# A hybrid transformer block: batch 0's residual, layer norm and first experts given out in attention a's last four periods

## The chip, the cores and the metric

The kernel runs on one core of one Trainium2 chip. The metric is device time in microseconds for one launch, the median of several runs. All arithmetic is in float32; two of the matmul operands are stored in the fp32r form.

## What is computed

Input x has 2 batches of 512 positions and 512 channels. Four layers follow one another, each with a layer norm ahead of it and a residual around it:

```python
x = x + attn_a(layernorm(x))    # 32 heads of 128, 8 kv heads, weights as 4-bit codes and scales
x = x + ffn(layernorm(x))       # 8 experts of rank 64, the best 2 of a softmax gate
x = x + attn_b(layernorm(x))    # 32 heads of 16, 8 kv heads
x = x + ffn(layernorm(x))       # the same experts again

def ffn(x):                     # x as 1024 rows
    gate_probs = softmax(x @ gate_w.T)
    weights, sel = top_k(gate_probs, 2)
    weights = weights / sum(weights)
    w_full = zeros(T, N_EXPERTS).at[arange(T)[:, None], sel].add(weights)
    for e in range(N_EXPERTS):
        out = out + w_full[:, e:e + 1] * (x @ lora_A[e].T @ lora_B[e].T)
```

Both attentions are causal and rotary. The change touches the place where the first line ends and the second begins.

## The kernel before

A program (a tile framework) assigns semaphores and places. It also orders the instructions on each engine when the kernel is built: in program order by preference, with later work drawn forward where its operands are there and the engine would be free. In the loop of attention b, TensorE's order is fixed by hand instead. Tiles come from pools; a pool's tag has a number of buffers, and pools opened later may lie on the place of pools that have been closed.

**Attention a** (lines 128 to 378). A unit is one head of one batch: 64 units in the order group g, batch b, head h, so units 60 to 63 are batch 1's last four and 56 to 59 batch 0's. The loop at line 335 has 68 periods. Period n gives out, in turns of one step each (`in_turn`, line 302), the following work on different units: `weighted` for unit n-3 (four groups of transposes L275 with their copies L276, then the av group of eight matmuls L280), `rotated` for unit n (query projection L209 and L210, evicted by L214 and L216, and the rotary L225 to L228), `output` for unit n-4 (L289 and L290, added to `acc` by L296 to L299), `softmaxed` for unit n-2 (scores L247, maxima L250 on VectorE, exponentials L255 on ScalarE, scaling L264 on GpSimd), and some steps of keys and values of the next group. From period 64 there are no projections any more, from 66 no scores, and period 67 has only the outputs of unit 63. `acc[0]`, batch 0's sum, is complete after period 63.

The pools of attention a, in order: `w` (4 buffers of converted weights, queries and outputs of two groups), `wkv` (2, keys and values), `xa` (the normalised input in two parts, and `acc`), `kv`, `tabs`, `rope` (tags rq, rsq, part and others), `qT`, `p`, `pT`, `attnT`; in PSUM two banks each of `ps_mm` (projections), `ps_sc` (scores), `ps_tp` and `ps_o`.

**Between.** After the loop the residual is added (L375 transposes `acc`, L376 adds it to x), for batch 0 and then batch 1. The pools of attention a are closed, and those of the rest opened: `w2` with `gw`, `fold`, the expert weights `la` and `lb`, and attention b's weights `wq2`, `wkv2`, `wo2` and `tabb`, loaded by SyncE's queue (L386 to L410); the padded tiles for queries, keys and values, cleared by GpSimd (L426 to L432).

**Experts and attention b.** `experts(b, which, store)` is a generator whose steps are: layer norm (`norm_parts`: one step with the statistics L460 and L461, the square root L463, then four tiles with L470, transposes L475 and copy L476), gate (`pg`, L494), first rank block (`ph`, L504, four steps), gate logits and softmax (`lg`, L514 to L521), the choice of two (L529 to L546, all on VectorE), three more rank blocks (twelve steps), the weights spread over the ranks and transposed (`we` L552, `wT` L556, L558; four steps), and the second matmul (`py`, L563, sixteen steps, with the addition to x at L567). Each is 43 steps. First `experts(0, "f1", False)` runs alone (line 784). Then `projections(0)` of attention b is given out in turn with `experts(1, "f1", False)`, which goes on as side work in attention b's loop, at a pace of 1.35 units a step.

```python
    run(experts(0, "f1", False))

    later, now = experts(1, "f1", False), projections(0)
    parts(later, 1)
    while next(now, None) is not None:
        parts(now, 1)
        parts(later, 1)
```

Of the kernel before, what the change touches and what calls it, by code (L numbers as in the profile page):

```python
# [11 lines left out]
F32 = mybir.dt.float32  # L12
I32 = mybir.dt.int32
F32R = mybir.dt.float32r
AF = mybir.ActivationFunctionType
# [26 lines left out]
def kernel(  # L42
# [80 lines left out]


# [3 lines left out]
    with ExitStack() as actx:  # L128
        wpool = actx.enter_context(tc.tile_pool(name="w", bufs=4))
        wkvp = actx.enter_context(tc.tile_pool(name="wkv", bufs=2))  # L130
# [7 lines left out]
        atp = actx.enter_context(tc.tile_pool(name="attnT", bufs=2))  # L138
        ps_mm = actx.enter_context(tc.tile_pool(name="ps_mm", bufs=2, space=PSUM))
        ps_sc = actx.enter_context(tc.tile_pool(name="ps_sc", bufs=2, space=PSUM))  # L140
        ps_tp = actx.enter_context(tc.tile_pool(name="ps_tp", bufs=2, space=PSUM))
        ps_o = actx.enter_context(tc.tile_pool(name="ps_o", bufs=2, space=PSUM))
# [57 lines left out]
        acc = {b: xp.tile([P, NC, S], F32, tag=f"acc{b}", name=f"acc_{b}") for b in range(B)}  # L200
# [105 lines left out]

        kTs, vs = {}, {}
# [27 lines left out]
        for n in range(len(units) + 4):  # L335
# [30 lines left out]
            turn.append(some(more, 3 + (units[min(n, 63)][0] == 0)))  # L366
            in_turn(*turn)

        for b in range(B):
            load_x("r", b, big, "big")  # L370
        for b in range(B):
            for t in range(NT):
                tp = ps_tp.tile([P, NC, P], F32, tag="tp", name=f"px_{b}_{t}")
                for n in range(NC):
                    nc.tensor.transpose(tp[:, n, :], acc[b][:, n, ts(t, P)], ident)  # L375
                nc.vector.tensor_tensor(  # L376
                    x[b, t], x[b, t], tp.rearrange("p n f -> p (n f)"), ALU.add
                )
# [4 lines left out]

    gw = w2.tile([P, NC, STRIP], F32, tag="gw", name="gw")
    nc.gpsimd.memset(gw, 0.0)
    nc.sync.dma_start(gw[:, :, :NE], gate_w)  # L386

    fold = w2.tile([P, NE], F32, tag="fold", name="fold")
    nc.vector.tensor_reduce(
        fold, ident.rearrange("p (c e) -> p e c", e=STRIP)[:, :NE, :], AX.X, ALU.add  # L390
    )
    la = w2.tile([P, NC, NE * RANK], F32, tag="la", name="la")
    nc.sync.dma_start(la, lora_a.rearrange("(c p) n -> p c n", p=P))
    lb = w2.tile([P, NC, DM], F32, tag="lb", name="lb")
    nc.sync.dma_start(lb, lora_b.rearrange("(c p) n -> p c n", p=P))
# [3 lines left out]
    nc.sync.dma_start(wkv2, wkv_b.rearrange("(c p) n -> p c n", p=P))  # L399

# [7 lines left out]

    tabb = w2.tile([P, NT, 4, B_HD], F32, tag="tabb", name="tabb")
    nc.sync.dma_start(tabb, rope_b)  # L410

# [24 lines left out]
    gate = ctx.enter_context(tc.tile_pool(name="gate", bufs=1))  # L436
# [6 lines left out]
    ps_f = ctx.enter_context(tc.tile_pool(name="ps_f", bufs=2, space=PSUM))  # L443

    shared = {"on": True}

    def bank(shape, name):
        pool, tag = (ps_x, "x") if shared["on"] else (ps_f, "f")
        return pool.tile(shape, F32, tag=tag, name=name)

    MM = 0.9
    def norm_parts(b, which):

        var = small.tile([P, NT, 2], F32, tag="mv", name=f"mv_{which}_{b}")
        for t in range(NT):
            st = small.tile([P, 6], F32, tag="st", name=f"st_{which}_{b}_{t}")
            nc.vector.bn_stats(st, x[b, t])  # L460
            nc.vector.bn_aggr(var[:, t, :], st)  # L461
        std = small.tile([P, NT], F32, tag="std", name=f"std_{which}_{b}")
        nc.scalar.activation(std, var[:, :, 1], AF.Sqrt, bias=eps)  # L463
        rstd = small.tile([P, NT], F32, tag="rstd", name=f"rstd_{which}_{b}")
        nc.vector.reciprocal(rstd, std)
        yield 7.0
        xT = xtp.tile([P, NC, S], F32, tag="xnT", name=f"xnT_{which}_{b}")
        for t in range(NT):
            xn = temps.tile([P, DM], F32, tag="t", name=f"xn_{which}_{b}_{t}")
            nc.vector.tensor_scalar(  # L470
                xn, x[b, t], var[:, t, 0:1], rstd[:, t : t + 1], ALU.subtract, ALU.mult
            )
            pt = bank([P, NC, P], f"pxT_{which}_{b}_{t}")
            for c in range(NC):
                nc.tensor.transpose(pt[:, c, :], xn[:, ts(c, P)], ident)  # L475
            nc.scalar.copy(xT[:, :, ts(t, P)], pt)  # L476
            yield MM
        return xT

    def experts(b, which, store):  # L480

        xT = yield from norm_parts(b, which)
        nm = f"{which}_{b}"

        def st(tag, n=1):
            return gate.tile([P, NT, n], F32, tag=tag, name=f"{tag}_{nm}")

        def each(a):
            return a.to_broadcast([P, NT, NE])


        pg = bank([P, S], f"pg_{nm}")
        for c in range(NC):
            nc.tensor.matmul(pg[ts(c, STRIP)], gw[:, c, :], xT[:, c, :], start=True, stop=True)  # L494
        shares = temps.tile([P, S], F32, tag="t", name=f"shares_{nm}")
        nc.scalar.copy(shares, pg)
        yield MM
        hT = hp.tile([P, NC, S], F32, tag="hT", name=f"hT_{nm}")

        def ranks(er):  # L500

            ph = bank([P, S], f"ph_{nm}_{er}")
            for c in range(NC):
                nc.tensor.matmul(  # L504
                    ph, la[:, c, ts(er, P)], xT[:, c, :], start=(c == 0), stop=(c == NC - 1)
                )
                if c == NC - 1:
                    nc.scalar.copy(hT[:, er, :], ph)
                yield MM

        yield from ranks(0)
        lg = bank([P, NT, NE], f"lg_{nm}")
        for t in range(NT):
            nc.tensor.matmul(lg[:, t, :], shares[:, ts(t, P)], fold, start=True, stop=True)  # L514
        mx, pr, den, rden = st("gmx"), st("gp", NE), st("gden"), st("grden")
        nc.vector.tensor_reduce(mx, lg, AX.X, ALU.max)
        nc.vector.tensor_tensor(pr, lg, each(mx), ALU.subtract)
        nc.scalar.activation(pr, pr, AF.Exp)
        nc.vector.tensor_reduce(den, pr, AX.X, ALU.add)
        nc.vector.reciprocal(rden, den)  # L520
        nc.vector.tensor_tensor(pr, pr, each(rden), ALU.mult)  # L521
        yield MM


        best, hot = [], []
        left = pr
        for n in range(2):
            m, key, km, oh = st(f"m{n}"), st(f"key{n}", NE), st(f"km{n}"), st(f"oh{n}", NE)
            nc.vector.tensor_reduce(m, left, AX.X, ALU.max)  # L529
            nc.vector.tensor_tensor(key, left, each(m), ALU.is_equal)  # L530
            nc.vector.tensor_tensor(
                key, key, order.unsqueeze(1).to_broadcast([P, NT, NE]), ALU.mult
            )
            nc.vector.tensor_reduce(km, key, AX.X, ALU.max)
            nc.vector.tensor_tensor(oh, key, each(km), ALU.is_equal)
            best.append(m)
            hot.append(oh)
            if n == 0:
                left = st("left", NE)
                nc.vector.scalar_tensor_tensor(left, oh, -2.0, pr, ALU.mult, ALU.add)  # L540
        tot, rtot, w = st("tot"), st("rtot"), st("gw", NE)
        nc.vector.tensor_tensor(tot, best[0], best[1], ALU.add)
        nc.vector.reciprocal(rtot, tot)
        nc.vector.tensor_tensor(w, hot[0], hot[1], ALU.add)
        nc.vector.tensor_tensor(w, w, pr, ALU.mult)
        nc.vector.tensor_tensor(w, w, each(rtot), ALU.mult)  # L546
        for er in range(1, NC):
            yield from ranks(er)
        for t in range(NT):

            we = wep.tile([P, NE, RANK], F32, tag="we", name=f"we_{nm}_{t}")
            nc.gpsimd.tensor_copy(we, w[:, t, :].unsqueeze(2).to_broadcast([P, NE, RANK]))  # L552
            wef = we.rearrange("p e r -> p (e r)")
            tp = bank([P, NC, P], f"wT_{nm}_{t}")
            for er in range(NC):
                nc.tensor.transpose(tp[:, er, :], wef[:, ts(er, P)], ident)  # L556
            part = hT[:, :, ts(t, P)]
            nc.vector.tensor_tensor(part, part, tp, ALU.mult)  # L558
            yield MM
        for t in range(NT):  # L560
            py = bank([P, DM], f"py_{nm}_{t}")
            for c in range(NC):
                nc.tensor.matmul(  # L563
                    py, hT[:, c, ts(t, P)], lb[:, c, :], start=(c == 0), stop=(c == NC - 1)
                )
                if c == NC - 1:
# [368 lines left out]
```

## Time and profile before

| | |
|---|---|
| median of 3 runs | 1170.47 us (1168.96 to 1172.08) |
| the profiled execution: time | 1172.71 us |
| the profiled execution: span of the core | 1170.7 us |
| TensorE (PE) busy | 1107.2 us, 95% of the span |
| VectorE (DVE) busy | 883.0 us, 75% |
| ScalarE (ACT) busy | 591.7 us, 51% |
| GpSimd (POOL) busy | 525.5 us, 45% |
| mean granted TensorE clock | 0.975 |

All durations come from the profiled execution. A span is from its first to its last instruction; times such as "at 722.3" are microseconds from the span's start. PEld is the weight load, which runs beside matmuls. One float32 matmul is two instructions in the trace. In rows of groups and chains, L504 is line 504 of the kernel, "x8" the number of instructions, and the two numbers ahead are start and length. In rows of stretches the number in brackets counts instructions, and the last three are clock, DMA share and GB/s. In rows of waits, the numbers are the sum, the number of waits, and the longest.

### The profile page before, as it was taken

To read this page: it belongs to the slowest core of one execution; us is meant where nothing else is said; L and a number is where in the kernel's file an instruction comes from. 1 tells how busy PE (TensorE), PEld (TensorE's weight loads), DVE (VectorE), ACT (ScalarE), POOL (GpSimd) and SP (SyncE) were. 2 spreads that over 40 slices of the span, in tenths; PEclk is the share of its full clock that TensorE was granted. 3 is DMA by queue.
4 is the path that set the end of the run, shared out by engine and by line. 5 is a ranking of instruction groups with operands and counts; after the bars stand their busy time and mean duration, and the time that the engine had idled before them with its cause. 6 is when DMAs were issued, how large, how long until landed. Compare 5 with 4: busy or idle time off the path is not lost.

```text
span 1170.7 us, 16843 instructions
## 1 busy us (share of the span) xinstructions
PE 1107.2 (95%) x5428; PEld 694.0 (59%) x5428; DVE 883.0 (75%) x2175; ACT 591.7 (51%) x1373; POOL 525.5 (45%) x758
## 2 busy tenths in 40 slices
PE   5799999999999999999999996989999999999998
PEld 3467777777777776777777774444444444444343
DVE  6889899998998999999998887244755676565442
ACT  3566566576656656656566663212254444364410
POOL 1556655665565666566565665111123322222200
PEclk9999999999999999999999998899989978989999
DMA  7301011022001100101100002400000000000000
GB/s 274 108 1 37 1 37 37 1 72 72 3 35 37 37 1 37 38 1 37 37 1 1 1 1 92 76 0 1 2 1 6 6 6 6 7 6 2 15 32 36
DMA packets 13448, 35.07 MB, mean 30 GB/s; under 512 B 4081, under 2 KB 5041, under 8 KB 10801
## 3 DMA queue, kind: packets, MB, share of 16 engines
q1 hardware_dynamic: 13360, 34.01, 8.8%
q8 instruction: 43, 0.70, 0.2%
q14 instruction: 45, 0.36, 0.1%
HBM read 30.72 MB, written 2.10 MB: 28 GB/s over the span
## 4 chain that ended last, share of the span: by engine, by line
PE 86%; DVE 7%; ACT 2%; POOL 2%; issue 2%; DMA 1%; SPq 0%; DVEq 0%; ACTq 0%; POOLq 0%
PE av L280 11%; PE sc L247 11%; PE st_b L694 7%; PE tp L275 6%; PE ps_o L289 5%; PE ps_o L290 5%; PE ps_q L209 5%; PE py_f L563 5%; PE ps_q L210 5%; PE ph_f L504 4%; PE num_b L721 4%; PE po L764 3%; PE pq_b L603 3%; PE sc_b L668 2%; PE ps_k L210 1%
## 5 line engine op out<-in xcount | busy, mean ns | idle before, releaser
L672 DVE CUSTOM_DVE_ANT_0 sc_b<-sc_b,tri 128x128 f32<-128x128 f32 (+3 forms) x256 | 122.6, 510 | 92.2 <-PE sc_b L668 76.6
L255 ACT ACTIVATE p<-sc,nmx 128x128 f32<-128x128 f32 (+3 forms) x256 | 135.5, 529 | 93.9 <-DVE nmx L250 91.8
L247 PE MATMUL sc<-kT,qT 128*128 128x128 f32 (+3 forms) x512 | 179.6, 433 | 1.5 <-POOL qT L228 1.2
L216 DVE SCALAR_TENSOR_TENSOR r_q<-ps_q,s_q,r_q 128x512 f32<-128x512 f32 x192 | 143.7, 749 | 35.8 <-PE ps_q L210 22.4
L227 POOL TENSOR_TENSOR r_q<-r_q,tab 128x512 f32<-128x512 f32 x64 | 82.3, 1286 | 191.1 <-DVE rs_q L226 191.1
L276 ACT COPY pT<-tp 128x128 f32<-128x128 f32 (+3 forms) x256 | 109.3, 427 | 102.2 <-PE tp L275 101.5
L264 POOL TENSOR_SCALAR p<-p,rden 128x128 f32<-128x128 f32 (+3 forms) x256 | 139.2, 556 | 46.2 <-DVE rden L262 22.8
L704 POOL TENSOR_SCALAR_AFFINE_SELECT pT_b<-pT_b 128x128 f32<-128x128 f32 (+1 forms) x192 | 62.7, 331 | 195.2 <-ACT pT_b L700 192.5
L280 PE MATMUL av<-pT,v 128*128 128x512 f32 (+3 forms) x512 | 148.7, 433 | 0.2 <-ACT pT L276 0.2
L280 PEld LDWEIGHTS av<-pT,v 128*128 128x128 f32 x512 | 96.8, 190 | 80.6 <-issue 52.7
L700 ACT ACTIVATE pT_b<-st_b 128x384 f32<-128x384 f32 (+1 forms) x192 | 92.2, 528 | 96.3 <-PE sc_b L668 68.1
L299 DVE SCALAR_TENSOR_TENSOR acc<-ps_o,s_o,acc 128x512 f32<-128x512 f32 x186 | 137.7, 740 | 2.9 <-PE ps_o L290 2.7
L209 PE MATMUL ps_q<-xh,w_q 128*128 128x512 f32 x256 | 122.8, 480 | 7.4 <-DVE r_q L216 7.4
L250 DVE CUSTOM_DVE_ANT_0 sc<-sc,tri 128x128 f32<-128x128 f32 (+3 forms) x256 | 125.7, 491 | 3.5 <-PE sc L247 2.5
L694 PE MATMUL st_b<-qT_b_p,kT_b 32*128 32x256 f32 (+3 forms) x512 | 119.1, 503 | 6.0 <-DVE qpad L672 3.6
L668 PE MATMUL sc_b<-kT_b,qT_b_m 32*128 32x384 f32 (+3 forms) x512 | 118.2, 499 | 1.4 <-ACT qT_b_m L639 0.7
L275 PE MATMUL tp<-ident,p 128*128 128x128 f32 x640 | 112.7, 272 | 2.3 <-POOL p L264 2.3
L247 PEld LDWEIGHTS sc<-kT,qT 128*128 128x128 f32 x512 | 95.3, 189 | 24.3 <-POOL qT L228 1.6
L289 PE MATMUL ps_o<-ah,w_o 128*128 128x512 f32 x256 | 108.3, 424 | 1.1 <-ACT ah L168 0.9
L290 PE MATMUL ps_o<-al,w_o 128*128 128x512 f32 x256 | 103.4, 407 | 3.5 <-DVE al L169 3.5
L210 PE MATMUL ps_q<-xl,w_q 128*128 128x512 f32 x256 | 101.5, 396 | 0.0
L275 PEld LDWEIGHTS tp<-ident,p 128*128 128x128 f32 x640 | 82.8, 140 | 28.9 <-issue 4.8
(175 smaller groups left out, 2010.6 us busy)
## 6 DMA issues: line engine op xcount, KB each, us to landing
codes_q<-in_q_codes_dram SPq DMA_DIRECT2D x8, 1024.0 KB, 4.8
codes_o<-in_o_codes_dram SPq DMA_DIRECT2D x8, 1024.0 KB, 4.8
x_a<-in_x_dram SPq DMA_DIRECT2D x8, 256.0 KB, 6.6
codes_k<-in_k_codes_dram SPq DMA_DIRECT2D x2, 1024.0 KB, 6.3
codes_v<-in_v_codes_dram SPq DMA_DIRECT2D x2, 1024.0 KB, 6.0
x_r<-in_x_dram SPq DMA_DIRECT2D x8, 256.0 KB, 3.5
out_dram<-x_r SPq DMA_DIRECT2D x8, 256.0 KB, 2.1
la<-in_lora_a_dram SPq DMA_DIRECT2D x1, 1024.0 KB, 5.6
```

The costliest lines, as they stand in the source:

```text
L209: nc.tensor.matmul(ps, w[:, c, ts(h, A_HD)], xh[b][:, c, :], start=True, stop=False)
L210: nc.tensor.matmul(ps, w[:, c, ts(h, A_HD)], xl[b][:, c, :], start=False, stop=True)
L216: nc.vector.scalar_tensor_tensor(r, ps, s, r, ALU.mult, ALU.add)
L247: nc.tensor.matmul(sc[:, :n], qT[:, ts(i, P)], kT[:, :n], start=True, stop=True)
L264: nc.gpsimd.tensor_scalar(prs[j], prs[j], rden[:, j % 2 : j % 2 + 1], 1.0, ALU.mult, ALU.mult)
L275: nc.tensor.transpose(tp[:, j, :], prs[i][:, ts(j, P)], ident)
L280: nc.tensor.matmul(av[:, j * P :], v[:, j, :], pT[:, j, j * P :], start=(j == 0), stop=(j == NT - 1))
L289: nc.tensor.matmul(ps, w[:, h, ts(n, P)], ah, start=True, stop=False)
L290: nc.tensor.matmul(ps, w[:, h, ts(n, P)], al, start=False, stop=True)
L299: nc.vector.scalar_tensor_tensor(to, ps, s, to, ALU.mult, ALU.add)
L668: nc.tensor.matmul(part, qT[strip, ts(i, P)], kT[strip, kh, :n], start=True, stop=True)
L694: nc.tensor.matmul(st[:, at : at + n], kT[strip, kh, ts(j, P)], qT[strip, j * P :], start=True, stop=True,)
```

## The change

`place`, `norm_parts`, `experts`, `gw` and `fold` move to the front of the kernel, and what they use (where xT, hT, xn, we and the PSUM banks lie) is looked up in `homes` and `banks`. At period 60 the x tiles for the residual, `gate_w` and both expert weights are loaded; the weights go into the two buffers of `wkv`. From period 64 on, each turn of the four last periods also gives out two steps of `early`: batch 0's residual (`added(0)`) and then `experts(0)`. xT and hT lie in buffers of `w`, xn and shares in those of rq, we in those of rsq, the banks in turn in `ps_mm` and `ps_sc`. What is left of `early` after period 67 is given out in turn with batch 1's residual. `acc` has a pool of its own, and the order of the pools is changed: `xa`, `kv`, `tabs`, `rope`, `qT`, `p`, `pT`, `attnT`, `acc`, `wkv`, `w`, and in PSUM `ps_tp`, `ps_o`, `ps_mm`, `ps_sc`. The expert weights are loaded a second time, into `w2`, for batch 1 and the second experts. Batch 1's experts give out six steps instead of one ahead of attention b's projections. The bodies of `norm_parts` and `experts` are otherwise as before.

```diff
+    homes, banks, lora = {}, [], {}
+
+    def place(kind, shape, name):
+        if kind == "bank":
+            pool, tag = banks[0]
+            banks.append(banks.pop(0))
+        else:
+            pool, tag = homes[kind]
+        return pool.tile(shape, F32, tag=tag, name=name)
+
+    gw = const.tile([P, NC, STRIP], F32, tag="gw", name="gw")
+    nc.gpsimd.memset(gw, 0.0)
+
+    fold = const.tile([P, NE], F32, tag="fold", name="fold")
...
+    gate = ctx.enter_context(tc.tile_pool(name="gate", bufs=1))
+
+    def load_lora(pool, tags):
+        for k, src in (("a", lora_a), ("b", lora_b)):
+            if k in tags:
+                lora[k] = pool.tile([P, NC, DM], F32, tag=tags[k], name=f"lora_{k}")
+                nc.sync.dma_start(lora[k], src.rearrange("(c p) n -> p c n", p=P))
...
     with ExitStack() as actx:
-        wpool = actx.enter_context(tc.tile_pool(name="w", bufs=4))
-        wkvp = actx.enter_context(tc.tile_pool(name="wkv", bufs=2))
+
         xp = actx.enter_context(tc.tile_pool(name="xa", bufs=1))
...
+        accp = actx.enter_context(tc.tile_pool(name="acc", bufs=1))
+        wkvp = actx.enter_context(tc.tile_pool(name="wkv", bufs=2))
+        wpool = actx.enter_context(tc.tile_pool(name="w", bufs=4))
+        ps_tp = actx.enter_context(tc.tile_pool(name="ps_tp", bufs=2, space=PSUM))
+        ps_o = actx.enter_context(tc.tile_pool(name="ps_o", bufs=2, space=PSUM))
         ps_mm = actx.enter_context(tc.tile_pool(name="ps_mm", bufs=2, space=PSUM))
         ps_sc = actx.enter_context(tc.tile_pool(name="ps_sc", bufs=2, space=PSUM))
...
+        def added(b):
+
+            for t in range(NT):
+                tp = place("bank", [P, NC, P], f"px_{b}_{t}")
+                for n in range(NC):
+                    nc.tensor.transpose(tp[:, n, :], acc[b][:, n, ts(t, P)], ident)
+                nc.vector.tensor_tensor(
+                    x[b, t], x[b, t], tp.rearrange("p n f -> p (n f)"), ALU.add
+                )
+                yield
+
+        def paired(stage):
+
+            for _ in range(4):
+                next(stage, None)
+                next(stage, None)
+                yield
...
             turn.append(some(more, 3 + (units[min(n, 63)][0] == 0)))
+            if n == 60:
+
+
+                nc.sync.dma_start(gw[:, :, :NE], gate_w)
+                load_lora(wkvp, {"a": "w", "b": "w"})
+                for b in range(B):
+                    load_x("r", b, big, "big")
+                homes.update(xT=(wpool, "w"), hT=(wpool, "w"), xn=(rp, "rq"), we=(rp, "rsq"))
+                banks[:] = [(ps_mm, "mm"), (ps_sc, "sc")]
+                early = chain(added(0), experts(0, "f1", False))
+            if n >= 64:
+                turn.append(paired(early))
             in_turn(*turn)
-
-        for b in range(B):
-            load_x("r", b, big, "big")
-        for b in range(B):
-            for t in range(NT):
-                tp = ps_tp.tile([P, NC, P], F32, tag="tp", name=f"px_{b}_{t}")
...
+        in_turn(added(1), early)
 
 
     xtp = ctx.enter_context(tc.tile_pool(name="xnT", bufs=2))
     w2 = ctx.enter_context(tc.tile_pool(name="w2", bufs=1))
...
+    load_lora(w2, {"a": "la"})
     wq2 = w2.tile([P, NC, DM], F32, tag="wq2", name="wq2")
     nc.sync.dma_start(wq2, wq_b.rearrange("(c p) n -> p c n", p=P))
     wkv2 = w2.tile([P, NC, 256], F32, tag="wkv2", name="wkv2")
     nc.sync.dma_start(wkv2, wkv_b.rearrange("(c p) n -> p c n", p=P))
+
+    tabb = w2.tile([P, NT, 4, B_HD], F32, tag="tabb", name="tabb")
+    nc.sync.dma_start(tabb, rope_b)
+    load_lora(w2, {"b": "lb"})
...
+    homes.update(xT=(xtp, "xnT"), xn=(temps, "t"), hT=(hp, "hT"), we=(wep, "we"))
+
+    ALONE, BESIDE = [(ps_x, "x")], [(ps_f, "f")]
+    banks[:] = ALONE
...
-    run(experts(0, "f1", False))
 
     later, now = experts(1, "f1", False), projections(0)
-    parts(later, 1)
+    parts(later, 6)
     while next(now, None) is not None:
```

## The prediction, made before the change was run

> **What bounds the kernel now.** I read the page's busy shares and slices first, to see which engine carries the span and where it fails to.
>
> ```profile
> PE 1107.2 (95%) x5428; PEld 694.0 (59%) x5428; DVE 883.0 (75%) x2175; ACT 591.7 (51%) x1373; POOL 525.5 (45%) x758
> PE   5799999999999999999999996989999999999998
> PEclk9999999999999999999999998899989978989999
> ```
>
> TensorE is busy nearly everywhere except at both ends and in slices 25 to 27 (702 to 790 us): there attention a ends and the change acts. So next the busy time by stretches, cut at the ends of a's last periods, which the chain shows as its groups of eight L280 matmuls (columns: stretch, length, busy PE, PEld, DVE, ACT, POOL, then clock, DMA share, GB/s).
>
> ```profile
> 690.70:698.35 7.65, 7.65 (x37) 5.01 (x36) 5.42 (x16) 5.00 (x14) 5.96 (x8) 1.00 0.00 0
> 698.35:706.05 7.70, 7.70 (x35) 4.94 (x34) 5.20 (x14) 5.00 (x14) 3.46 (x6) 1.00 0.00 0
> 706.05:712.90 6.85, 5.97 (x29) 4.06 (x29) 2.88 (x4) 2.77 (x6) 2.26 (x3) 1.00 0.00 0
> 712.90:717.65 4.75, 4.25 (x24) 2.73 (x22) 3.89 (x7) 2.56 (x3) 1.28 (x1) 1.00 0.01 3
> 717.65:728.30 10.65, 2.94 (x16) 2.02 (x17) 10.51 (x26) 0.59 (x2) 6.96 (x10) 0.65 0.43 141
> 728.30:741.00 12.70, 11.91 (x41) 6.36 (x42) 2.81 (x4) 3.61 (x7) 5.36 (x24) 0.62 1.06 247
> 741.00:767.60 26.60, 26.22 (x72) 12.05 (x72) 10.94 (x34) 4.45 (x6) 2.33 (x4) 1.00 0.07 10
> ```
>
> Periods 64 and 65 (first two rows) have a full PE, so work put there isn't hidden: it lengthens them. The room is in the rows after. Which waits make it, from the list of waits in 688 to 770 us and, last row, in 770 to 950 us:
>
> ```profile
> PE pxT_f L475 <- DVE xn_f L470: 6.1, 1, 6.1
> PE px L375 <- DVE x_r L376: 1.7, 2, 1.5
> PE ps_o L289 <- ACT ah L168: 0.9, 2, 0.6
> PE pxT_b L475 <- DVE xn_b L470: 3.2, 2, 2.9
> ```
>
> The 6.1 us is batch 0's layer norm, waited for with nothing else to do. The chain of waits then gives PE's own prices: at the low clock (first two rows) and at full clock.
>
> ```profile
> 733.25 1.93 PE pg_f L494 x8
> 735.18 5.02 PE ph_f L504 x8
> 740.99 10.40 PE ph_f L504 x24
> 753.85 13.75 PE py_f L563 x32
> 771.59 0.87 PE pxT_b L475 x8
> 778.61 1.00 PE pg_f L494 x8
> 792.50 0.79 PE lg_f L514 x8
> ```
>
> **The change part by part.** *PE's sum.* From 690.70 (period 64 begins) to 767.60 (batch 0's last py_f) are 76.9 us. The work in it at full clock: periods 64 and 65 as they are, 15.35; period 66 ten transposes (1.1), eight output matmuls of 0.233 (1.9) and the av group (2.16), 5.1; period 67's outputs 1.9; 32 px transposes at 0.109, 3.5; 16 pxT_f 1.75; pg_f 1.0; 32 ph_f at 0.433, 13.9; lg_f 0.8; 16 wT_f 1.75; py_f 13.75. Together 58.8, so 18.1 us are waits and low clock. The change removes no work; it can win at most these 18.1 here.
>
> *Where the steps fall.* The early generator has 47 steps: 4 px, 1 of statistics, 4 xn, pg, 4 ranks, lg, 12 ranks, 4 wT, 16 py. Eight per period take 32: period 64 gets 4 px, the statistics and 3 xn, period 65 up to the first step of the second rank, 66 eight rank steps, 67 the rest to the first py. Fifteen py steps follow, beside batch 1's px. PE's load: period 64 7.65+28x0.109 = 10.7; 65 7.7+0.44+1.0+0.8+5x0.867 = 14.3; 66 5.1+6.9 = 12.0; 67 1.9+2.6+1.75+0.9 = 7.1; then 13.0+1.75. That is again 58.8, ending at 749.5 if PE never waits.
>
> *Period 64, DVE.* It has 5.2 of its own (second row). Added: four x additions of 0.68; four pairs of statistics, 0.66 from start to start around 725 us; a reciprocal 0.2; three xn. L470 took 0.54 at 770 us but 3.90 for four, 0.97 each, beside POOL's memsets at 727; POOL now runs its p scalings beside them. So 5.2+2.7+2.7+0.2+1.6 = 12.2, or 13.5 with the slow xn, against PE's 10.7. DVE sets this period: 1.5 to 2.8 lost, less what PE's spare banks absorb, so 0 to 3; I take 2.5, since attention's L250 queues behind this work and p, then the next period's transposes, wait for L250.
>
> *ACT's table.* The norm's square root stands among attention's exponentials: one switch to it and one back. The row of before is 1283 ns a switch, and the exponential at 742.19 starts as the load from 740.90 ends. The Trainium skill, "ScalarE: Activation LUTs", section "What ACT_TABLE_LOAD costs", adds about 1380 ns of drain, 2.66 us a switch, and advises batching by table set, which speaks against this change. By the row ACT has 5.0+2x1.28+0.3+3x0.58 = 9.6 in period 64, below PE's 10.7: nothing. By the page it has 12.4: up to 1.7 lost, and my gain would be 13. I take the row; no drain shows there. The number of switches up to batch 1's experts stays four (before: 715.9, 740.9, 752.0, 792.1). What queues behind the square root on ACT, waiting for DVE's statistics, are pT copies and p; that is part of the 2.5.
>
> *Periods 65 to 67.* pg_f waits for xn, transpose and copy of the last tile, about 0.54+0.44+0.58, with attention's matmuls to cover most: 0.7. wT_f waits for POOL's four we copies (0.61 each, two buffers): before, the 1.75 took 2.5, so 0.7. The banks of ps_sc that ph_f holds for two turns leave softmax one: its round trip of matmul, L250 and p is about 2 us against 3.5 a turn, nothing; bound 0 to 1. Batch 1's px waits for the last acc (0.75): 0.6 with what else is late. Holes together 2.5+0.7+0.7+0.6 = 4.5; 18.1-4.5 = 13.6.
>
> *Queues and places.* At period 60 SP issues gate_w, lora_a, lora_b and eight x loads; SP is empty from 575.6 to 722.3 and the DMA share there is 0.00 to 0.01. lora_a and lora_b are now loaded twice, 2 MB more; landing took 5.6 and 7.5 us, use comes 30 us later: nothing. gw's memset (0.2) and fold (0.2) go to the start, where POOL waits 8.3 us for codes and DVE 3.8 for x: nothing. In the trace gw and the weights start at 722.3, when the last px ends: acc lay under w2, and a new pool waits for whole old pools. After the change w2 lies on xa, kv, tabs, rope, qT and p; the last of these in use is rope (shares and we), free when wT_f is done, near 737. Then la (5.6 us), wq (9.9), wkv (12.9) land beside the 14.75 us of py and px, and POOL's pad memsets (10.7 us) run there too. Cost nothing while that cover holds; 3 to 5 if the place comes free only with py's end.
>
> *After py.* Before, PE waited 2.9 us for batch 0's second norm (fourth wait). Now six steps of batch 1's experts are given out first: pxT_f and pg_f are 2.75 us, and ranks follow. I count 2.5 won; bounds 0 to 2.9. Those six steps instead of one also move five rank steps (4.3 us) ahead of the attention-b loop. They are conserved, but the loop's side work (62.7 units at 1.35 a step) ends near step 43 instead of 46, and steps without side work take about 2 us instead of 2.9 (around 940 us): 3.3 steps save 3.0, so 1.3 lost.
>
> Sum: 13.6+2.5-1.3 = 14.8 us. Against the profiled execution (1172.71, span 1170.7) that is 1157.9; it ran 2.2 above the median, so the median goes from 1170.47 to about 1156.
>
> **The rivals.** *A, half of it comes back (1163).* The places come late (3 to 5 us), or DVE's chain stalls softmax in two periods rather than one (3 more): gain 7. For: DVE is over PE in period 64 and the six pads plus weights were all late together at 722. Against: over periods 64 and 65 DVE has about 22.5 to 23.8 and PE 25.0, so DVE catches up.
>
> *B, no waits (1150).* Banks absorb period 64 and batch 1's ranks fill everything after py: 18.1+2.9-1 = 20. For: the scheduler already hoists px and statistics into holes (712.7, 714.5). Against: DVE's load.
>
> *C, slower (1178).* The clock. In period 64 or 65 PE waits as long as it did before pxT_f (6.1 us) and its clock falls while attention and batch 0 still have some 44 us of matmuls ahead. A matmul microsecond at 0.6 costs 0.67 more. Before, the clock stayed near 0.62 from 717 to 741. The page "TensorE: Matmul & The Clock Gate", section "Part 1: The HAM clock gate", has it halve after an idle window of about 3.4 us and return after as much sustained work: by the page C costs 6.1+1.7 = 8, still a gain of 7; by the row, 20 us of PE work in the slow state cost 13 more. It ends slower when over about 13 us of work run at 0.6 besides the stall: with 25 us, 6.1+16.7 = 23, so 8 slower. Against: PE always has attention's matmuls between the links of the chain, so I see stalls of 2 to 3 us.
>
> *D, nothing (1170).* The steps only lengthen full periods and the end waits as before: it needs the scheduler to keep batch 0's chain for the end. The generators' order is against it.
>
> **How the numbers follow.** The likeliest case, 1156 (own range 1151 to 1160), has 0.62; A 0.20 (1160 to 1167); B 0.09 (1147 to 1151); D 0.04; C 0.05. A measurement of this kernel tells about 0.3% from no change, 3.5 us. Faster by more (under 1167): 0.62+0.09+0.19 = 0.90; within: D and A's edge, 0.05; slower 0.05. The range reaches from B's better half to most of A: 1149 to 1165.
>
> **What would show it.** In the changed profile: PE busy and clock 1.00 without a gap from 690 to about 753, the 6.1 us wait gone; period 64 at 12 to 14 us, 65 to 67 near 15, 12.5 and 8; two table loads between 690 and 705; la, wq and wkv issued near 737 and landed before 754; py_f ending near 754 instead of 767.6. Wrong would be a clock below 1 in 690 to 740, weights issued after py_f, or a loop of attention b longer by what the front won.

## The result, and the profile after

The changed kernel takes 1155.17 us in the median of 4 runs (1151.10 to 1156.43), the kernel before beside it 1171.28 (1168.96 to 1174.74). The ratio is 0.9849 with a 95% interval of 0.9821 to 0.9877: 1.5% faster. The prediction was 1156, with 1149 to 1165 as its range. The profiled execution took 1154.85 us, its span is 1153.1 us.

The busy shares, and the slices of TensorE and its clock, from the page of the changed kernel:

```profile
PE 1101.1 (95%) x5428; PEld 693.6 (60%) x5428; DVE 881.1 (76%) x2175; ACT 592.0 (51%) x1373; POOL 526.9 (46%) x758
...
PE   4799999999999999999999999998999999999898
...
PEclk8999999999999999999999999999989988989999
```

The dip that slices 25 to 27 had in PE and in the clock is gone (each slice is now 28.8 us, so these are 692 to 778 us). PE issues the same 5428 instructions. So the time came from waits and low clock.

The front, from the start of period 64 to batch 0's last py_f, as one stretch each: the kernel before, the changed kernel, and the changed kernel run again (e8, below). The number behind the length is PE's busy time, the third from the end the clock:

```profile
690.70:767.58 76.88, 66.63 (x247) 37.18 (x245) 41.65 (x103) 23.98 (x51) 27.61 (x53) 0.89 0.26 64
690.07:753.16 63.09, 61.23 (x248) 36.47 (x248) 42.17 (x106) 23.60 (x51) 26.55 (x52) 0.97 0.21 66
690.89:752.91 62.02, 59.93 (x248) 35.01 (x248) 41.99 (x106) 23.57 (x51) 26.53 (x52) 1.00 0.22 68
```

Length less busy time is what PE stands still: 10.25 us before, 1.86 and 2.09 after. At a clock of 1.00 throughout (e8) the matmuls are busy for 59.93 us; what the other two rows have above that goes with their lower clock. So of the 13.8 us of the first two rows, 8.4 are idle time and 5.4 matmuls that ran at a higher clock.

The front of the changed kernel by stretches, cut at the ends of the periods (stretch, length, busy PE, PEld, DVE, ACT, POOL with counts, granted clock, DMA share, GB/s). Period 65 is in two rows:

```profile
690.07:699.49 9.42, 9.35 (x51) 6.74 (x50) 9.05 (x24) 4.33 (x12) 5.82 (x7) 1.00 0.00 0
699.49:702.83 3.34, 1.71 (x7) 0.89 (x6) 2.42 (x8) 3.21 (x5) 0.00 (x0) 0.98 0.00 0
702.83:718.99 16.16, 16.16 (x71) 10.32 (x72) 8.03 (x27) 8.67 (x22) 4.90 (x7) 0.90 0.00 1
718.99:730.99 12.00, 12.00 (x43) 6.78 (x43) 4.66 (x16) 3.94 (x8) 2.41 (x3) 1.00 0.00 0
730.99:737.67 6.68, 6.52 (x31) 4.15 (x31) 3.83 (x6) 3.15 (x4) 2.41 (x3) 1.00 0.00 0
737.67:753.16 15.49, 15.49 (x51) 7.59 (x50) 14.17 (x29) 0.30 (x1) 11.01 (x32) 1.00 0.87 269
```

One hole is left, the second row, where PE is busy for 1.71 of 3.34 us. The list of waits for 688 to 770 us of the changed kernel (waited for: us in total, times, longest) shows how small the rest is:

```profile
PE ps_o L439 <- DVE acc L449: 1.0, 1, 1.0
PE pg_f L193 <- ACT xnT_f L175: 0.9, 1, 0.9
PE ps_o L439 <- ACT ah L318: 0.6, 1, 0.6
...
PE wT_f L255 <- POOL we_f L251: 0.2, 1, 0.2
```

The 6.1 us before pxT_f are gone, and so are the 2.9 before pxT_b; 0.9 before batch 1's pg_f has taken their place. The chain of waits of the changed kernel at the hole, and later where batch 0's experts end (start us, us, what):

```profile
700.34 0.21 ACT L162
700.55 1.09 issue
701.63 0.30 ACT std_f L162
701.96 0.18 DVE rstd_f L164
702.14 0.65 DVE acc L449
702.83 0.79 PE ps_o L439
...
742.86 10.30 PE py_f L262 x24
```

The last 24 py_f take 10.30 us, 0.43 each, at full clock. The first six lines are the hole. ScalarE loads the square root's table for 1.28 us (the first two lines), and the deviation follows it. VectorE takes the reciprocal, and only then the `acc` sum queued behind it (L449), although that sum needs neither. The output matmul L439 waits for the bank which that sum frees.

The table lists each stage in one profile per kernel, in us. The front is as above, period 64 beginning with the end of the av group of period 63; "idle" is PE's idle time in the front, "clock" the clock there; "up to sc_b" runs on to attention b's first score; the loop from there to the first reciprocal of its denominators. The profile is of the slowest run of its kernel for e1, e2, e3 and e4 (1.5 to 5.6 us above the median), and of the fastest for e6 and e8 (3.1 and 1.8 below).

| kernel | start of front | front | idle | clock | up to sc_b | loop | rest |
|---|---|---|---|---|---|---|---|
| before | 690.7 | 76.9 | 10.25 | 0.89 | 44.2 | 134.0 | 224.8 |
| changed | 690.1 | 63.1 | 1.86 | 0.97 | 45.7 | 130.7 | 223.5 |
| changed, run again (e8) | 690.9 | 62.0 | 2.09 | 1.00 | 45.7 | 129.7 | 224.0 |
| e1: no steps in the periods | 691.9 | 70.4 | 5.83 | 0.95 | 47.2 | 132.4 | 223.7 |
| e5: as e1, batch 1's residual first | 691.5 | 69.7 | 7.15 | 0.98 | 48.8 | 130.9 | 223.7 |
| e9: as e5, pads and weights beside the norm | 690.1 | 73.6 | 8.48 | 0.93 | 47.1 | 132.4 | 223.6 |
| e2: one step ahead | 690.5 | 63.2 | 1.87 | 0.97 | 44.2 | 135.1 | 227.2 |
| e3: no table switch | 690.4 | 61.8 | 2.03 | 1.00 | 45.7 | 132.3 | 223.7 |
| e4: from period 66 | 691.5 | 65.8 | 3.36 | 0.97 | 47.4 | 130.9 | 223.9 |
| e6: weights' place free late | 690.3 | 62.0 | 2.09 | 1.00 | 47.6 | 128.3 | 222.9 |
| e7: 1, 2, 3, 3 steps a turn | 692.2 | 63.6 | 2.06 | 0.97 | 45.7 | 129.8 | 223.7 |

Between the first two rows: 0.6 earlier (nothing in the change explains it), 13.8 from the front, 1.5 given back up to sc_b, 3.3 from the loop, 1.3 from the rest, which is not explained either; 17.6 us of span in all.

### The profile page after: what moved, and what is told of

Its sections match the earlier page's. It is cut to its first block, busy times and chain, and to the rows that moved or that the text cites. A ratio compares the mean times of both kernels' runs of the same rounds, so it can differ in the third digit from the quotient of the medians.

```text
span 1153.1 us, 16828 instructions
## 1 busy us (share of the span) xinstructions
PE 1101.1 (95%) x5428; PEld 693.6 (60%) x5428; DVE 881.1 (76%) x2175; ACT 592.0 (51%) x1373; POOL 526.9 (46%) x758
## 4 chain that ended last, share of the span: by engine, by line
PE 85%; DVE 8%; ACT 2%; issue 2%; DMA 1%; POOL 1%; SPq 1%; DVEq 0%; ACTq 0%; POOLq 0%
PE av L430 11%; PE sc L397 11%; PE st_b L728 7%; PE tp L425 5%; PE py_f L262 5%; PE ps_o L440 5%; PE ps_o L439 5%; PE ps_q L359 5%; PE ps_q L360 5%; PE ph_f L203 5%; PE num_b L755 3%; PE po L798 3%; PE sc_b L702 3%; PE pq_b L637 3%; PE pkv_b L645 1%
## 5 line engine op out<-in xcount | busy, mean ns | idle before, releaser
L449 DVE SCALAR_TENSOR_TENSOR acc<-ps_o,s_o,acc 128x512 f32<-128x512 f32 x186 | 137.4, 739 | 5.9 <-PE ps_o L440 5.8
L702 PE MATMUL sc_b<-kT_b,qT_b_m 32*128 32x128 f32 (+3 forms) x512 | 119.0, 497 | 2.6 <-DVE qpad L706 1.5
L439 PE MATMUL ps_o<-ah,w_o 128*128 128x512 f32 x256 | 108.4, 424 | 1.7 <-DVE acc L449 1.0
```

What stands on the lines that cost most here:

```text
L439: nc.tensor.matmul(ps, w[:, h, ts(n, P)], ah, start=True, stop=False)
L449: nc.vector.scalar_tensor_tensor(to, ps, s, to, ALU.mult, ALU.add)
L702: nc.tensor.matmul(part, qT[strip, ts(i, P)], kT[strip, kh, :n], start=True, stop=True)
```

## The experiments

Kernels were timed beside the kernel before on the same chip, whose median there was 1173.16 (e1 to e4), 1173.67 (e5 to e8) and 1173.63 (e9). Where two variants lie close, their ratios to it are compared; 0.001 of ratio is 1.2 us.

### e1: nothing given out in the periods

```diff
-            if n >= 64:
-                turn.append(paired(early))
```

All else stays: the second copy of the expert weights, the homes of the tiles, four banks, six steps ahead.

> The changed kernel without giving the early steps out in periods 64 to 67: places, pools, loads and the six steps of batch 1 stay; batch 0's residual, norm and experts are given out after the loop. Theory (the gain is attention's matmuls covering the waits of batch 0's chain): the wait of about 6 us before pxT_f and the low clock are back, batch 0's last py_f ends near 765 us again, time 1167 (1165 to 1170). Rival (the gain comes from the new places, earlier weights and the six steps): 1155 to 1160, with clock 1.00 in 717 to 741.

It took 1165.08 us (1163.96 to 1167.24), ratio 0.9935 (0.9912 to 0.9959). The theory is nearer, but not all of it holds: the front is 70.4, so 6.5 of its 13.8 us remain without any step in the periods, and PE's idle time is 5.83 where the kernel before had 10.25. The timeline of PE in this kernel (start, us, instruction, in brackets the idle time before it and its releaser) shows the wait for the norm:

```profile
724.60 1.34 PE L174 MATMUL pxT_f<-ident,xn_f 128*128 128x128 f32 x8 [2.58 <-DVE xn_f L169]
...
728.79 1.94 PE L193 MATMUL pg_f<-xnT_f,gw 128*32 128x512 f32 x8 [0.68 <-ACT xnT_f L175]
```

It waits 2.58 us here, where the kernel before waited 6.1. Is that due to the order, or to the places? e5 and e9 ask this.

### e5: as e1, with batch 1's residual first

In e1 px of batch 1 falls between px of batch 0 and its norm. This puts it ahead, as before the change:

```diff
-                early = chain(added(0), experts(0, "f1", False))
+                early = experts(0, "f1", False)
...
-        in_turn(added(1), early)
+        in_turn(chain(added(0), added(1), early))
```

> As the first experiment (early steps after the loop), but batch 1's residual is given out ahead of batch 0's norm and experts, as in the kernel before, not in turn with them. Theory 1 (the 6.5 us that the first experiment kept at the front came from VectorE, which before put batch 1's residual and statistics ahead of batch 0's xn): the wait before pxT_f is back near 5 to 6 us and the time near 1170. Theory 2 (they came from the places: POOL's pad memsets and the weights no longer stand beside batch 0's norm, whose four xn took 3.9 us beside them): 1165 to 1167, as in the first experiment.

It took 1167.13 us (1165.57 to 1168.17), ratio 0.9948 (0.9927 to 0.9968). The front is 69.7, no longer than e1's. But the two fronts as one stretch each (e1, then e5) show two effects that cancel:

```profile
691.92:762.31 70.39, 64.56 (x249) 36.46 (x248) 41.84 (x106) 22.62 (x50) 26.43 (x52) 0.95 0.17 56
691.50:761.15 69.65, 62.50 (x248) 36.36 (x248) 41.84 (x106) 22.52 (x50) 26.43 (x52) 0.98 0.17 58
```

PE's idle time is 1.3 us longer in e5 (7.15 against 5.83), with a wait of 4.92 before pxT_f, near the 5 to 6 that the theory of the order had. The low clock was shorter in e5's profile (pg_f 1.07 us, below, against e1's 1.94). By the ratios e5 is 1.5 us slower, with intervals that overlap. So the order of batch 1's residual explains about 1.3 us of waiting, and not the 6.5. The rest of the 6.5 goes with what the change moved to other places, and with the clock.

### e9: as e5, with GpSimd's pads and the weights beside the norm again

Normalised tiles, shares and the spread weights (`we`) move from the rope pool to the one that holds `ah` and `al`. The rope pool's last use then comes earlier, and with it the start of `w2` and of the pads.

```diff
-  homes.update(xT=(wpool, "w"), hT=(wpool, "w"), xn=(rp, "rq"), we=(rp, "rsq"))
+  homes.update(xT=(wpool, "w"), hT=(wpool, "w"), xn=(atp, "ah"), we=(atp, "al"))
```

> As the fifth experiment (early steps after the loop, batch 1's residual first; VectorE's order of instructions is the same), but xn, shares and we lie in the buffers of attnT instead of rope's, so that attention b's pool is free when attention a's outputs end and POOL's pad memsets and the weights start near 719 us, beside batch 0's norm, as in the kernel before. Theory (of the 7.2 us that the front of the fifth experiment is shorter than before's, the memsets beside VectorE's norm make a good part): each xn takes 0.9 to 1 us instead of 0.5, the wait before pxT_f grows, and the front is 2 to 5 us longer than 69.65: 1169 to 1171. Rival (it is the banks and the expert weights that were there already): front 69 to 70, time 1166 to 1168.

It took 1169.69 us in 10 runs (1165.16 to 1170.76), ratio 0.9961 (0.9945 to 0.9977). The front is 4.0 us longer than e5's; in the whole time the medians differ by 2.6, by the ratios it is 1.5, and the intervals overlap. As one stretch, the front of e9 has 8.48 us of idle time, 1.3 more than e5's, and a lower clock:

```profile
690.10:763.73 73.63, 65.15 (x248) 36.85 (x248) 44.09 (x106) 22.73 (x50) 27.85 (x52) 0.93 0.26 67
```

The timelines show where the idle time comes from. First e5 (VectorE, then PE; no memset of the pads runs before 748.47):

```profile
724.50 0.98 DVE L169 TENSOR_SCALAR xn_f<-x_r,mv_f,rstd_f 128x512 f32<-128x512 f32 x2
...
725.18 3.33 PE L174 MATMUL pxT_f<-ident,xn_f 128*128 128x128 f32 x16 [4.92 <-DVE xn_f L169]
729.18 1.07 PE L193 MATMUL pg_f<-xnT_f,gw 128*32 128x512 f32 x8 [0.68 <-ACT xnT_f L175]
730.18 3.70 PE L203 MATMUL ph_f<-xnT_f,lora_a 128*128 128x512 f32 x8
```

Then e9 (VectorE, PE, GpSimd):

```profile
723.11 2.40 DVE L169 TENSOR_SCALAR xn_f<-x_r,mv_f,rstd_f 128x512 f32<-128x512 f32 x2
...
724.49 2.26 PE L174 MATMUL pxT_f<-ident,xn_f 128*128 128x128 f32 x8 [5.62 <-DVE xn_f L169]
727.24 2.29 PE L174 MATMUL pxT_f<-ident,xn_f 128*128 128x128 f32 x8 [0.50 <-DVE xn_f L169]
730.20 1.94 PE L193 MATMUL pg_f<-xnT_f,gw 128*32 128x512 f32 x8 [0.68 <-ACT xnT_f L175]
732.07 4.40 PE L203 MATMUL ph_f<-xnT_f,lora_a 128*128 128x512 f32 x8
...
717.75 7.48 POOL L582 MEMSET qpad<- 128x1024 f32 x8 [0.91 <-DVE acc L449]
```

VectorE's order is the same in both. In e9 two xn take 2.40 us beside the memsets, against 0.98. PE waits 5.62 and 0.50 us in place of 4.92: 1.2 of the 1.3. It then stays longer at the low clock: pg_f 1.94 against 1.07, eight ph_f 4.40 against 3.70. That part, 2.7 of the 4.0 us, can't be put down to the memsets: e1 has pg_f at 1.94 too, with no memset beside its norm. The kernel before ran as e9 does (its memsets began when px was done).

The weights' transfers run at the same time as the memsets. The changed kernel tells the two apart, where batch 1's four xn run late beside the pads (the four with shortest, median and longest duration in ns, then a stretch in which GpSimd does nothing):

```profile
L169 DVE TENSOR_SCALAR xn_f<-x_r,mv_f,rstd_f x4: 527/535/1834, 748.1 to 750.8; 128x512 f32<-128x512 f32 x4
749.90:751.30 1.40, 1.40 (x5) 0.58 (x4) 1.40 (x5) 0.00 (x0) 0.00 (x0) 1.00 1.14 316
```

The first, at 748.14, takes 1.83 us beside the last memsets; from 749.9 on they are done, the DMA share is still 1.14, and an xn takes 0.53. So it is the memsets.

### e4: steps from period 66 only, twice as many

```diff
-                next(stage, None)
-                next(stage, None)
+                for _ in range(4):
+                    next(stage, None)
...
-            if n >= 64:
+            if n >= 66:
```

> The changed kernel with the early steps given out four a turn in periods 66 and 67 only. Theory (PE's work is conserved and only waits count): periods 64 and 65 are back at 7.65 us, and batch 0's norm chain of some 6 us starts beside period 66, which has only 5.1 us of matmuls of its own to cover it: 2 to 4 us lost, 1157 to 1159. Rival (work put into the full periods 64 and 65 is hidden there): 10 us or more lost, 1165.

It took 1155.63 us (1153.9 to 1161.27), ratio 0.9864 (0.9838 to 0.9890). The front is 65.8, 2.7 longer than the changed kernel's (3.8 than e8's), 1.3 to 1.5 of it idle time; but the profiled execution took 1161.27, 5.6 above the median. The median missed the expected 1157 to 1159: by the ratios e4 is 1.5 to 1.8 us slower than the changed kernel, with intervals that overlap. The rival's 1165 is out: the last two periods alone take most of the gain.

### e3: without the switch of ScalarE's table

Batch 0's norm in the first experts takes Identity in place of the square root, so its scale is another one; nothing else differs.

```diff
-        nc.scalar.activation(std, var[:, :, 1], AF.Sqrt, bias=eps)
+        nc.scalar.activation(std, var[:, :, 1],
+            AF.Identity if (b, which) == (0, "f1") else AF.Sqrt, bias=eps)
```

> The changed kernel with the identity in place of the square root in batch 0's first norm, so that ScalarE needs no table switch there; the instruction, its wait and its place stay, and the norm's scale is left wrong. Theory (the switch stands on the path: rstd waits on VectorE for it, L449 is queued behind rstd, and TensorE waits for that bank; 2 us lost between 699.5 and 702.8): 1.3 to 2.6 us shorter, 1152.5 to 1154. Rival (VectorE's own load sets that wait and the switch is hidden, as the prediction's sum of busy time had it): no change, 1155.

It took 1154.13 us (1153.27 to 1155.62), ratio 0.9844 (0.9818 to 0.9870), against 0.9849 and 0.9851 with the switches. Its front as one stretch:

```profile
690.37:752.13 61.76, 59.73 (x248) 35.21 (x248) 43.07 (x106) 21.05 (x49) 26.54 (x52) 1.00 0.22 67
```

PE's idle time is 2.03 us, against 1.86 and 2.09 with the switches. Against e8, whose clock was 1.00 too, the front is 0.3 us shorter; the 1.3 us against the first profile go with the lower clock there. So two switches are worth some 0.3 us here at most, which the total can't tell. ScalarE's timeline of the changed kernel shows them:

```profile
700.34 1.28 ACT L162 ACT_TABLE_LOAD   x1
701.63 0.30 ACT L162 ACTIVATE std_f<-mv_f,eps 128x4 f32<-128x4 f32 x1
701.95 1.28 ACT L405 ACT_TABLE_LOAD   x1
703.24 0.69 ACT L405 ACTIVATE p<-sc,nmx 128x512 f32<-128x512 f32 x1
```

Each activation starts as its load ends. And without the switch the hole stays about as long, as this stretch of e3 from the end of period 64 shows:

```profile
699.80:703.49 3.69, 2.24 (x12) 1.38 (x11) 3.34 (x10) 3.14 (x8) 0.79 (x2) 1.00 0.00 0
```

PE stands still for 1.45 us here, against 1.63 with the switches. e3's list of waits from 699 to 705 us names other links:

```profile
PE tp L425 <- POOL p L414: 0.6, 1, 0.6
PE ps_o L439 <- ACT ah L318: 0.6, 1, 0.6
PE ps_o L440 <- DVE al L319: 0.2, 1, 0.2
```

Take the table away, and attention's own softmax and output split, on engines that the norm's steps load, hold PE for about as long.

### e7: fewer steps in the periods where VectorE is full

```diff
-        def paired(stage):
+        def paired(stage, k):
...
-                next(stage, None)
-                next(stage, None)
+                for _ in range(k):
+                    next(stage, None)
...
-                turn.append(paired(early))
+                turn.append(paired(early, (1, 2, 3, 3)[n - 64]))
```

> The changed kernel with one early step a turn in period 64, two in 65, three in 66 and 67. Theory (VectorE is at its limit in period 64, 9.05 of 9.42 us busy, so that statistics end late and TensorE loses 2 us at the start of 65): the residual alone lies in 64, the statistics meet a VectorE with room in 65, and 1 to 2 us of the front's 4.3 are saved: 1153.5 to 1154.5. Rival (the chain's length costs the same wherever it starts): 1155 to 1157.

It took 1156.70 us (1154.57 to 1157.12), ratio 0.9857 (0.9832 to 0.9882). The expectation fell. The front is 63.6, and its stretches say why:

```profile
702.01:707.74 5.73, 4.14 (x24) 2.72 (x22) 5.12 (x16) 5.25 (x10) 2.14 (x3) 1.00 0.00 0
707.74:713.00 5.26, 5.26 (x21) 3.98 (x22) 2.24 (x6) 3.83 (x10) 0.99 (x2) 0.68 0.00 0
```

The hole moved with the statistics into period 65 (PE 4.14 of 5.73), and the clock fell to 0.68 behind it. PE's idle time in the front is 2.06, as long as before the move: the norm's chain has to pass somewhere.

### e6: the weights' place free only after py

Pool `w`, which now holds batch 0's transposed input and ranks, is opened first, so that `w2` comes to lie on it and waits for the last py_f.

```diff
+        wpool = actx.enter_context(tc.tile_pool(name="w", bufs=4))
         xp = actx.enter_context(tc.tile_pool(name="xa", bufs=1))
...
-        wpool = actx.enter_context(tc.tile_pool(name="w", bufs=4))
```

> The changed kernel with the pool of xT and hT opened first, so that the pool of attention b's weights and pads lies over it and becomes free only with batch 0's last py_f. Theory (the prediction's rival A: weights and memsets are covered only while they start near 738): lora_a lands 5 to 6 us after py_f, the wait after py_f grows by 3 to 5 us: 1158 to 1161. Rival (TensorE has enough other work or VectorE's chain is as long): 1155 to 1156.

It took 1155.94 us (1152.80 to 1156.43), ratio 0.9855 (0.9827 to 0.9884). The expectation fell. The first load on SyncE's queue, in the changed kernel:

```profile
738.65 0.37 SPq L148 DMA_DIRECT2D lora_a<-in_lora_a_dram  x1
```

In e6 the load is issued 14 us later, and the list of waits after py has one entry for it:

```profile
752.50 0.37 SPq L148 DMA_DIRECT2D lora_a<-in_lora_a_dram  x1
```

```profile
PE ph_f L203 <- DMA lora_a<-in_lora_a_dram: 1.2, 1, 1.2
```

The stage up to sc_b is 1.9 us longer (47.6 against 45.7), and the total doesn't show it: the loop of that profile, an execution of 1152.80, was 1.4 to 2.4 us shorter than those of the two runs of the changed kernel. Why is open.

### e2: one step of batch 1's experts ahead

```diff
-    parts(later, 6)
+    parts(later, 1)
```

> The changed kernel with one step of batch 1's experts ahead of attention b's projections, as before, instead of six. Theory by the sum on record: the wait of 2.9 us for batch 0's second norm is open again (+2.5), but five steps stay beside attention b (-1.3): 1156.4, within 1155 to 1159. Rival (the six steps bring nothing, since the waits only change places): 1154 to 1155.

It took 1159.09 us (1155.29 to 1161.82), ratio 0.9884 (0.9858 to 0.9909). PE's timeline has the old wait again ("issue": the profile names no releaser):

```profile
756.60 0.63 PE L174 MATMUL pxT_b<-ident,xn_b 128*128 128x128 f32 x4 [2.97 <-issue]
```

The stage up to sc_b is 44.2, as before the change, and the loop 4.4 longer than the changed kernel's: 2.9 us together. By the medians, each against its own kernel before, it is 2.0 to 3.8 (14.1 us gained, against 16.1 and 17.9), by the ratios 3.9 to 4.1. The direction is as expected, the size more than the 1.2 that the terms gave, but the intervals overlap. The rest of this profile, an execution of 1161.82, ran 3.7 longer, though the edit doesn't touch it; that is not explained.

### e8: the changed kernel once more

> The changed kernel again, to stand beside the three others on the same chip: 1155 (1153 to 1157).

It took 1155.77 us (1153.99 to 1157.08), ratio 0.9851 (0.9826 to 0.9877). This gives the scatter of the stages from one profile to the next: 1.1 us in the front and as much in the loop. In PE's idle time in the front it is 0.2. The hole has the same length, but the clock differs. Stretches from the end of period 64, first the changed kernel's first profile:

```profile
699.49:707.00 7.51, 5.88 (x26) 4.62 (x26) 5.42 (x16) 6.18 (x11) 1.54 (x2) 0.77 0.00 0
```

Then e8:

```profile
700.31:708.00 7.69, 5.83 (x34) 4.07 (x34) 5.87 (x16) 7.39 (x15) 2.56 (x3) 1.00 0.00 0
```

PE stands still for 1.6 and 1.9 us, and the clock granted is 0.77 in one and 1.00 in the other. At 0.77, 7.5 us lose up to 1.7 us of work.

## Why the prediction was right, and where it was not

**The sum.** Predicted 14.8 us: 13.6 from the front, 2.5 after py, less 1.3 in the loop. Measured in the two profiles: 13.8 from the front, and 3.3 less 1.5 = 1.8 from py_f to the loop's end, where 2.5 - 1.3 = 1.2 was forecast. The other 1.9 of the 17.6 us lie ahead of the front and in the rest, where nothing was forecast. The two parts after py_f are there, as the stage up to sc_b before and after shows:

```profile
767.58:811.82 44.24, 38.04 (x147) 21.60 (x146) 17.32 (x57) 10.91 (x27) 8.01 (x10) 1.00 0.00 1
753.16:798.90 45.74, 42.25 (x158) 23.41 (x155) 14.90 (x53) 11.91 (x29) 8.05 (x10) 1.00 0.12 16
```

PE's idle time fell from 6.2 to 3.5, 2.7 won, and its work rose by 4.2, the five rank steps counted as 4.3. The loop gave 3.3 back of that (4.4 in e8), 3.0 forecast. So the case named likeliest holds. Rivals A and D are out, and so is C as a whole; B's full 18.1 at the front wasn't reached.

**The holes: the number came out, its parts did not.** The prediction kept 4.5 us of holes, and 63.1 less its 58.8 us of work is 4.3. But PE stood still for 1.86 us only (2.09 in e8). The matmuls of the front took 59.93 us at a clock of 1.00 (e8), 1.1 more than the 58.8 (so the room was 17.0 and not 18.1), and the lower clock of the first profile added 1.3, which the prediction's likeliest case put at nothing. That these three errors nearly cancel is luck. In e8, without the low clock, the front won 14.9.

The place was wrong as well. The prediction had 2.5 of its holes in period 64, which it put at 12 to 14 us. Period 64 took 9.42 with PE full: no xn lies in it, and VectorE (9.05 busy) just fitted. The norm's chain came at the start of 65, which took 19.5 in place of 15. Period 66 took 12.0 with nothing lost, and 67 with py 22.2, of which PE stood still for 0.2, against 1.3 forecast.

**The clock.** A clock below 1 in 690 to 740 was named as a sign of being wrong. The first profile shows it: 0.77 over the 7.5 us from the hole's start (e8, above), which costs up to 1.7 us of work; in e8 it stayed at 1.00. What rival C had right is that the clock can fall in these periods; its stall of 6.1 us did not come.

**The table.** The prediction put its cost at nothing, since ScalarE's busy sum lay below PE's. The argument was not good enough: the first switch stands in the chain, at 700.34. The size of one was right: 1.28 us with no drain behind it, as in the row of before and not the 2.66 of the Trainium skill ("ScalarE: Activation LUTs", section "What ACT_TABLE_LOAD costs"; the advice to batch by set stands in another section of that page, "Table sets: the hidden batching unit"). And the switches are nearly free (some 0.3 us at most) for another reason: without them other links are late there, for 1.45 us in place of 1.63 (e3).

**What removed the 18.1.** The prediction gave all of it to one mechanism, attention's matmuls beside the norm. The runs split it. PE's idle time in the front, which scatters least, goes from 10.25 to 8.48 (e9), 7.15 (e5) and 1.86 or 2.09. So giving steps out in the periods is worth 5.1 to 5.3 us of it (3.7 to 4.0 counted from e1, where batch 1's residual covers part of the wait). 1.3 come with GpSimd's pads and the weights leaving the norm, which the prediction counted only as a possible cost. 1.8 come with the other places, four banks for px and the second copy of the expert weights among them; these were not separated. The rest of the front's 13.8 us is clock, which no run here assigns. In the whole time, by the ratios to the kernel before, the steps in the periods are worth 9.9 to 11.6 us of 17.5 to 17.7 (from e1 and e5), and the rest includes the six steps of batch 1. The shares are those of this order of undoing; how much of the 1.3 would be left once the steps are given out in the periods wasn't tried.

**Rival A's price.** "3 to 5 if the place comes free only with py's end" was too high: with exactly that, PE waited 1.2 us for the weights and the stage grew by 1.9. Batch 1's pxT_f, pg_f and the first pxT_b cover most of the landing.

## What to carry to other kernels

To ask whether a short step on an engine is hidden, follow what stands behind it in that engine's queue, not the engine's busy sum: here a reciprocal that waited for a table load held up a sum which freed PE's bank. When a stage is moved, list also what stops running beside it: of 8.3 us of idle time that went, some 3 came from other things than the work that was put under the matmuls. When a sum comes out right, compare its parts: here idle time, work and clock were each off by more than a microsecond. Where a chain of several engines has to pass once, moving it about (e7, e4) or shortening one link (e3) brings little, as the next link is late instead.

## What the runs showed of the hardware

A plain memset on GpSimd slows VectorE's tensor_scalar of 128x512 float32: 0.98 us for two with GpSimd idle (e5), 2.40 for the same two beside the memset (e9). Other work of VectorE is not slowed there: four additions of `px` to x (L463, 128x512, one operand in PSUM) take 2.48 us in e5 without and in e9 with the memsets beside them, two statistics (L159) 1.25 in both.

The clock is not a function of the idle time alone. The same hole, with 1.6 to 1.9 us of PE idle spread over 3.3 us, was followed by a clock of 0.77 in one run and 1.00 in another, and in e7, with 1.6 us of idle over 5.7 us, by 0.68. The page "TensorE: Matmul & The Clock Gate" of the Trainium skill, section "Part 1: The HAM clock gate", has the clock halve after an idle window of about 3.4 us; no single gap here was that long. The same section has the window run free of the kernel's start, so that the same hole can fall into it in different ways. That would fit, but no run here shows it.
